# Letting VectorE share GpSimd's products and bias rows, loading masks first, and choosing a planner's urgencies anew, in a four-block attention kernel

## The chip, the cores and the metric

The kernel runs on one core of a Trainium2 chip. The metric is the device time of one execution in microseconds (us), given as the median of several runs. A profile of one further execution comes with it. Its engines are PE (TensorE's matmuls), PEld (TensorE's weight loads), DVE (VectorE), ACT (ScalarE), POOL (GpSimd) and SP (SyncE, which here only issues transfers).

## The reference

Eight sequences of 128 tokens with 256 features go through four transformer blocks, L0 to L3, all in fp32. `ctx_2048` is a second set of eight sequences of the same shape. Cut to what matters:

```
L0: x += attention(norm(x), ctx, mask)    # 16 heads of 16, boolean mask over keys
    x += mlp(norm(x))                     # 256 -> 1024 -> 256
L1: attention of x over [ctx, x]          # integer mask over keys, no norm ahead of it
    x = that and an MLP of its norm
L2: x += wide_attention(norm(x), ctx)     # twice; 16 heads of 128, learned bias key/value
    x += mlp(norm(x))
L3: x += attention(norm(x), norm(x), ltor_mask)
    x += attention(norm(x), ctx, cross_mask)
    x += mlp(norm(x))

# L3's attention:
scores = einsum(q, k) / sqrt(16)
scores = scores * mask - 10000.0 * (1.0 - mask)
probs  = softmax(scores)
return einsum(probs, v)
```

Each attention and each MLP ends with a bias row of 256 numbers that is added to every token.

## The kernel before

**Threads.** The eight sequences are cut into five threads, T0 to T4, of 1, 1, 2, 2 and 2 sequences (`SIZES`). A thread is a chain of Python generators, `blocks(T)`, that goes through L0, L1, L2 and L3. Threads run beside each other, so that TensorE has the products of one while the others are in a softmax or a norm. At most three are in the first two blocks, and three in the wide one. The last thread is cut in two parts, one sequence each, for L3 (`BY_BATCH`, `Part`).

**The order.** No engine's order is written by hand. While the program is built, the class `Plan` plays the kernel through: it keeps a clock (`now`), a time until which each engine is taken (`until`), and a list of what the generators ask for. A generator yields `op(engine, f)`, or a sum of two of these where either engine may do the work. When an engine comes free, `_choose` gives it the most urgent thing that names it (the lowest number, then the oldest) and calls `f`, which emits the instructions. Engines are asked in the order PE, POOL, ACT, DVE, SP. How long an instruction takes on the planner's clock comes from `_weight`, which also tells whether a DVE instruction shares SBUF's port with POOL: then the planner starts it only when POOL is done (`_end`). Where TensorE would idle, the planner may put in a matmul on `ident` whose result nobody reads (`idle_work`).

**Urgencies.** The numbers in `U` belong to kinds of work (`'norm'`, `'mask'`, `'k'`, `'softmax'`, `'load'`, ...), and those in `LATE` are added for each thread and stage. Together they make the order. A wrong guess of the planner costs time on the chip, as each engine keeps to the emitted order.

**Transfers.** `load` asks SP for a transfer, or SP or ACT where it is marked `early`. `dma` places its landing on the planner's clock: `dma_until` is the time at which the transfers asked so far are through, 2500 ns at first, and each KB adds 2.8 ns. `inputs` asks for `x`, `ctxT` and the columns of biases and scales (`cols`) with urgency -3. `key_bias` loads the mask over keys with -1, on SP alone; from it DVE makes `hs`, `ms` and `kss`, ACT or POOL write biases into `k`, and DVE adds the keys of `ctx` to these.

**L3's softmax**, `by_pairs`, works on 128 queries x four heads x 128 keys at a time (a tile `t` of 128x512):

```
DVE   t = scores * mask                 (scores in PSUM)
POOL  t = t + (mask - 1) * -10000
DVE   mn = min of t
ACT   t = exp(mn - t), sums into sm     (four instructions)
DVE   sm = 1 / sm
POOL  t = t * sm                        ("the product with the inverse sums")
PE    transposes of t, then t times v
```

L2's softmax, `after_scores`, has such a product on POOL too; the profile names both `t<-t,sm`.

**Rows of biases.** `normed` loads the bias row that a stage adds at its end into `row`; `norm` starts `add_rows`, which adds it to the residual (`x<-x,row`) on POOL. The stage's last DVE addition, `x<-mm,x`, waits for this through `row_in`. In `norm` the case `w is None` is L1's attention, which has no norm: there the transposes read the residual itself.

Nearly every instruction is recorded at line 335, the call in `Engine`; groups are told apart by tile names.

Of the kernel before, what the change touches and what calls it, by code (L numbers as in the profile page):

```python
# [62 lines left out]
FRONTS, WIDES = 3, 3  # L63
BY_BATCH = (4,)
AHEAD = [[(1, 0), (1, 1)], [], [(1, 0)], [], []]
U = {'take': 0.75, 'taken': -1, 'norm': 1.33, 'mask': 5.29, 'k': 2.24, 'q': 0.77, 'v': 3.01, 'by key': 0.17, 'softmax': 1.71, 'weights': 1.17, 'pairs': 0.21, 'out': 0.57, 'mlp norm': -0.18, 'mlp 1': 2.92, 'mlp 2': 3.41, 'wide norm': 1.02, 'wide k': 3.4, 'wide q': 3.13, 'wide v': 5.44, 'wide s': 4.05, 'wide': 0.43, 'ahead': 3.67, 'load': -0.56, 'early': 0.98}
LATE = [(4.59, -1, -1, -0.66, 1.03, -1, 2.77, 3.05, 3.1, 3.0, 2.25, 1.84, 0.92), (16.8, 0.32, 4.0, 6.02, 1.18, -1, 3.37, 3.57, 8.14, 4.15, -0.94, 0.09, 0.94), (2.67, 10.11, 4.03, 1.81, 2.31, 3.16, 3.3, 3.73, 4.79, 13.74, 3.59, 9.93, 9.83), (4.81, 12.33, 4.01, -1, -0.06, 1.37, 3.1, -0.03, 1.5, 1.56, 0.96, -0.5, -1), (1.56, 2.64, -0.58, -0.46, 1.42, -0.16, 4.41, 1.29, 0.75, -1, -1, 3.81, -0.53)]


class Event:  # L70
# [14 lines left out]
class Plan:  # L85
# [12 lines left out]
    def __init__(self):  # L98
        self.now = 0
        self.seq = 0  # L100
        self.events = []
        self.asked = []
        self.until = {e: 0 for e in self.SEEN}
        self.weight, self.shared, self.wrote = 0, False, []
        self.idle_work = None
        self.both_until = {"DVE": 0, "POOL": 0}
        self.clock = Clock()
        self.count = 0
        self.log = []
        self.table = None  # L110
        self.dma_until = 2500
        self.live = {}

    def spawn(self, gen, urgency, after=0):
# [150 lines left out]
def _weight(eng, name, args, kw):  # L265

    aps = [x for x in (*args, *kw.values()) if isinstance(x, bass.AP)]
    sizes = [x.free_size() for x in aps]
    n = max(sizes)
    if name == "dma_start":  # L270
        return 480, False
    by_part = sum(m == 1 for m in sizes[1:]) if n > 2 else max(0, len(aps) - 2) if name == "tensor_scalar" else 0
    on_sbuf = all(x.space == bass.MemoryType.SB for x in aps)
    if eng == "PE":
        if name == "transpose":
            return 109, False
        lhsT = kw["lhsT"]
        cols = aps[0].free_size()
        if lhsT.shape[0] < P:
            return 0.539 * cols, False  # L280
        if lhsT.free_size() < P:
            return 0.494 * cols, False
        return max(225, 1.7 * cols), False
    if eng == "ACT":
        if "accum_out" in kw:
            return 385, False
        if name == "copy":
            return 61 + 0.824 * n, False
        return 127 + 0.805 * n + (35 if on_sbuf and n == 256 else 0) + (40 if isinstance(kw.get("bias"), bass.AP) else 0) + (
            90 if isinstance(kw.get("scale"), bass.AP) else 0), False  # L290
    if eng == "DVE":
        if name == "tensor_scalar" and n == 4 and len(aps) == 2 and len(args) > 5:
            return 145, False
        if name == "reciprocal":
            return 65 + 6.25 * n, False
        if name in ("bn_stats", "bn_aggr"):
            return (330 if name == "bn_stats" else 150), False
        if n <= 8:
            return 68 + 55 * max(0, len(aps) - 2) * (name == "tensor_scalar"), False
        if name in ("tensor_scalar", "tensor_copy") and on_sbuf:  # L300
            return 75 + 0.8 * n + 55 * by_part, True
        two = name in ("tensor_tensor", "scalar_tensor_tensor") and sum(
            x.space == bass.MemoryType.SB and x.free_size() > 1 for x in aps[1:]) == 2
        return 72 + 1.03 * n + 55 * by_part, two
    if name == "memset":
        return 20 + n, False
    if n <= 16:
        return 195 + 75 * by_part, False
    if name == "tensor_tensor":
        inner = any(x.ap[-1][0] == 0 for x in aps[1:])  # L310
        return 100 + (1.85 if inner else 2.3) * n, False
    return (150 + 3.0 * n, 10 + 3.6 * n, 5 * n - 20)[by_part], False
# [34 lines left out]
def op(eng, f, lat=None, table=None):  # L347
    return ((eng, 0, f, lat, table),)
# [8 lines left out]
def four_blocks(ctx: ExitStack, tc: tile.TileContext, a: dict, out: bass.AP):  # L357
# [79 lines left out]
    def dma(f, kb_, early):  # L437

        def sync():
            f(nc.sync)  # L440
            plan.weight += max(0, plan.dma_until - plan.now - 3500)

        yield op("SP", sync) + (op("ACT", lambda: f(nc.scalar)) if early else ())
        plan.dma_until = max(plan.dma_until, plan.now) + kb_ * 2.8
        yield plan.dma_until - plan.now + 2300

    def load(dst, src, kb_, early=False):
# [189 lines left out]
    def norm(T, src, e, w, b, adds, rows, hT, ready, row_done, urgency):  # L637
# [4 lines left out]
        else:  # L642
# [48 lines left out]
                    nc.vector.tensor_scalar(xn[:, i, :], src[:, i, :], y[:, i, :], z[:, i, :], ALU.mult, ALU.add)  # L691

            yield from each(*(either(lambda i=i: scaled_act(i), lambda i=i: scaled_dve(i)) for i in range(nb)))
        spawn(add_rows(adds, rows, row_done, nb), urgency)
        yield (tl, 1)
        pt = bank("tl")[:, : NC * T.nt].rearrange("p (c b k) -> p c b k", c=NC, b=nb)

# [3 lines left out]
                    nc.tensor.transpose(pt[:, c, i, :], xn[:, i, c * P : (c + 1) * P], ident)  # L701

        yield op("PE", transposes)

        def out_act(c):
            to, s = hT[:, c, :], pt[:, c].rearrange("p b k -> p (b k)")
# [21 lines left out]
    def add_rows(adds, rows, row_done, nb):  # L728
        for (dst, src, _), (r, e) in zip(adds, rows):
            yield e  # L730
            yield op("POOL", lambda: nc.gpsimd.tensor_tensor(
                dst, src, r.unsqueeze(1).to_broadcast([P, nb, D]), ALU.add))
            plan.put(row_slots)
        plan.set(row_done)

# [72 lines left out]
    def key_bias(mask, dst, hs, ks, ks_in, name, dtype, T, may_be_none):  # L808

        nb = T.nb
        raw = mask[:, 0].bitcast(dtype)[:, :, :P]
        m = mask[:, 1]
        ms = new(act, [P, 2, nb], "ms", bufs=4)
        kss = new(act, [P, 2, NC, nb], "kss", bufs=4)
        yield spawn(load(raw, a[name][:, T.tokens].rearrange("o (b k) -> o b k", k=P).partition_broadcast(P), 64 * nb), -1)
        some = new(act, [P, nb], "some", bufs=4)

        def minus():
            nc.vector.tensor_scalar(m, raw, 0.0, -BIG, ALU.is_equal, ALU.mult)
            if may_be_none:
                nc.vector.tensor_reduce(some, m, AX.X, ALU.max)
                nc.vector.tensor_scalar(some, some, -1.0, None, ALU.is_ge)
            else:
                nc.vector.memset(some, 1.0)
            for e in range(2):
                nc.vector.tensor_scalar(hs[:, e], some, half[e], None, ALU.mult)
                nc.vector.tensor_scalar(ms[:, e], some, mask_row[e], None, ALU.mult)  # L830

        def biases():
            for e in range(2):
                for c in range(NC):
                    nc.vector.tensor_scalar(kss[:, e, c], some, ks[:, e, c : c + 1], None, ALU.mult)

        yield op("DVE", minus)
        yield ks_in
        yield op("DVE", biases)
        yield from each(*(  # L840
            op("ACT", lambda e=e, c=c, b=b: nc.scalar.activation(
                dst[:, e, c, b, 0, :], m[:, b], AF.Identity, bias=kss[:, e, c, b : b + 1], scale=ms[:, e, b : b + 1]))
            + op("POOL", lambda e=e, c=c, b=b: nc.gpsimd.tensor_scalar(
                dst[:, e, c, b, 0, :], m[:, b], ms[:, e, b : b + 1], kss[:, e, c, b : b + 1], ALU.mult, ALU.add))
            for e in range(2) for c in range(NC) for b in range(nb)))
# [253 lines left out]
    def by_pairs(T, ns, scale, mask, masks, q, k, v, v_in, vb, attnT):  # L1099
# [24 lines left out]
        def softmax(s, b, r, mn, sm, ts):  # L1124
# [12 lines left out]
            def exps():  # L1137
# [5 lines left out]
            yield op("ACT", exps, None, EXP)  # L1143
            yield op("DVE", lambda: nc.vector.reciprocal(sm[:, r], sm[:, r]))
            yield op("POOL", lambda: nc.gpsimd.tensor_tensor(
                t, t, sm[:, r].to_broadcast([P, 4, P]), ALU.mult))

        def values(b, soft, ts, turn, next_turn):
            yield turn
# [342 lines left out]
    def inputs():  # L1492
        for T in threads:
            h = T.h
            early = h < 2
            rows = (load(T.x, a["x"][T.batches].rearrange("b p d -> p b d"), 128 * T.nb, early),
                    load(T.ctx, a["ctxT"].rearrange("(c p) t -> p c t", p=P)[:, :, T.tokens], 128 * T.nb, early))
            for f, then in zip(rows, (T.ready, ctx_in[h])):
                spawn(all_then([spawn(f, -3)], then), 0)
            if h == 0:  # L1500
                spawn(all_then([spawn(load(cols, a["cols"], 140, True), -3)], cols_in), 0)
                first = new(const, [P, 1], "first")
                spawn(asks(op("ACT", lambda: nc.scalar.activation(first, ident[:, :1], AF.Exp), None, EXP)), 9)
            spawn(blocks(T), 0)
            yield 4000 if h == 0 else 8000
# [46 lines left out]
```

## Time and profile before

| | |
|---|---|
| median of 3 runs | 1195.21 us (1195.16 to 1196.08) |
| profiled execution, its own time | 1194.78 us |
| its span, first to last instruction | 1193.0 us |
| mean granted TensorE clock | 0.993 |
| PE busy | 1150.5 us (96%) |
| DVE, ACT, POOL busy | 798.8, 596.3, 360.4 us |
| moved by the transfers | 181.09 MB, 152 GB/s on average |
| POOL `t<-t,sm`, 128x512 | 128 times, 1041 ns each |
| POOL `t<-t,mask`, 128x512 | 64 times, 1276 ns each |
| POOL `x<-x,row` | 48 times, 999 ns each, over two sizes |

A busy share is an average over the whole span; what a change in one stage is worth shows only in that stage's stretch. The digits in the profile's second part are the busy share of 40 equal slices of the span, in tenths. In a group's row the columns are the engine, the operation, the tiles written and read, shapes and count; then the busy time in us and the mean ns of one; then the time in which the engine idled just before them, and what ended it. A row of the timeline has the start and length in us, and in brackets how long the engine stood idle before it and whose end released it. SPq and ACTq are the engines' issue of transfers.

### The profile page before, as it was taken

To read this page: it belongs to the slowest core of one execution; us is meant where nothing else is said; L and a number is where in the kernel's file an instruction comes from. 1 tells how busy PE (TensorE), PEld (TensorE's weight loads), DVE (VectorE), ACT (ScalarE), POOL (GpSimd) and SP (SyncE) were. 2 spreads that over 40 slices of the span, in tenths; PEclk is the share of its full clock that TensorE was granted. 3 is DMA by queue.
4 is the path that set the end of the run, shared out by engine and by line. 5 is a ranking of instruction groups with operands and counts; after the bars stand their busy time and mean duration, and the time that the engine had idled before them with its cause. 6 is when DMAs were issued, how large, how long until landed. Compare 5 with 4: busy or idle time off the path is not lost.

```text
span 1193.0 us, 23579 instructions
## 1 busy us (share of the span) xinstructions
PE 1150.5 (96%) x8816; PEld 956.5 (80%) x8816; DVE 798.8 (67%) x2186; ACT 596.3 (50%) x1538; POOL 360.4 (30%) x446
## 2 busy tenths in 40 slices
PE   7999999999999999999999999999999999988978
PEld 6677788888888878887887878888787778877767
DVE  6867568747776586787477265556855657678972
ACT  3555455355445374557353343633553336367872
POOL 2211211223124253013202022412532226165770
PEclk8999999999999999999999999999999999998999
DMA  9754567787645554435334534446443564351120
GB/s 299 219 162 136 160 201 214 238 273 229 190 143 196 152 185 145 135 112 147 117 116 141 165 106 145 124 131 187 138 137 122 139 183 133 117 143 55 32 85 19
DMA packets 134706, 181.09 MB, mean 152 GB/s; under 512 B 8896, under 2 KB 83392, under 8 KB 134592
## 3 DMA queue, kind: packets, MB, share of 16 engines
q1 hardware_dynamic: 133344, 178.55, 48.7%
q8 instruction: 70, 1.15, 0.4%
q10 hardware_dynamic: 1248, 1.03, 0.3%
q14 instruction: 44, 0.36, 0.1%
HBM read 178.50 MB, written 1.05 MB: 151 GB/s over the span
## 4 chain that ended last, share of the span: by engine, by line
PE 79%; DVE 11%; ACT 5%; DMA 2%; issue 1%; POOL 0%; SPq 0%; ACTq 0%; POOLq 0%; DVEq 0%
PE mm L335 57%; PE tl L335 17%; PE sc L335 5%; DVE rz L335 2%; ACT kb L335 1%; DVE t L335 1%; DMA w<-in_L_wk 1%; DMA bb<-in_L_bias_v 1%; ACT t L335 1%; DVE mn L335 1%; ACT q L335 1%; DVE ry L335 1%; ACT pt L335 1%; DVE kb L335 1%; DVE q L335 1%
## 5 line engine op out<-in xcount | busy, mean ns | idle before, releaser
L335 PE MATMUL mm<-hT,w 128*128 128x256 f32 (+1 forms) x1576 | 292.4, 335 | 12.0 <-ACT kb L335 2.5
L335 PEld LDWEIGHTS mm<-hT,w 128*128 128x128 f32 x1576 | 242.8, 191 | 43.5 <-issue 8.0
L335 POOL TENSOR_TENSOR t<-t,sm 128x512 f32<-128x512 f32 x128 | 132.0, 1041 | 298.5 <-DVE sm L335 242.8
L335 PE MATMUL mm<-ctxT,w 128*128 128x256 f32 (+1 forms) x768 | 148.7, 342 | 1.7 <-DVE x L335 0.8
L335 PE MATMUL mm<-w,ctxT 128*128 128x512 f32 (+1 forms) x352 | 145.9, 542 | 4.6 <-DMA w<-in_L_v_w 2.0
L335 PEld LDWEIGHTS mm<-ctxT,w 128*128 128x128 f32 x768 | 121.7, 194 | 16.5 <-issue 3.0
L335 PE MATMUL mm<-w,at 128*128 128x256 f32 x512 | 121.5, 380 | 0.2 <-DVE kb L335 0.2
L335 PE MATMUL mm<-w,kb 128*128 128x256 f32 x512 | 119.6, 382 | 0.9 <-PE mm L335 0.8
L335 POOL TENSOR_TENSOR x<-x,row 128x256 f32<-128x256 f32 (+1 forms) x48 | 48.0, 999 | 232.7 <-ACT xn L335 108.3
L335 PEld LDWEIGHTS mm<-w,at 128*128 128x128 f32 x512 | 94.7, 190 | 16.2 <-issue 2.6
L335 ACT ACTIVATE t<-t,mn 128x128 f32<-128x128 f32 x256 | 99.5, 395 | 12.8 <-DVE mn L335 11.6
L335 PEld LDWEIGHTS mm<-w,kb 128*128 128x128 f32 x512 | 94.1, 190 | 14.6 <-PE mm L335 1.4
L335 DVE TENSOR_TENSOR x<-mm,x 128x256 f32<-128x256 f32 (+1 forms) x102 | 47.6, 466 | 82.8 <-PE mm L335 82.1
L335 POOL TENSOR_TENSOR t<-t,mask 128x512 f32<-128x512 f32 x64 | 80.2, 1276 | 63.9 <-DVE t L335 62.5
L335 PEld LDWEIGHTS mm<-w,ctxT 128*128 128x128 f32 x352 | 63.0, 192 | 42.7 <-issue 33.6
L335 POOL TENSOR_TENSOR bv<-bv,bb 128x512 f32<-128x512 f32 x40 | 50.8, 1271 | 153.2 <-DMA bb<-in_L_bias_v 137.0
L335 ACT ACT_TABLE_LOAD x60 | 77.0, 1283 | 15.5 <-PE sc L335 6.7
L335 ACT ACTIVATE at<-tl,cols 128x128 f32<-128x128 f32 x212 | 60.4, 371 | 46.5 <-PE tl L335 46.2
L335 PE MATMUL tl<-ident,t 128*128 128x128 f32 x512 | 75.5, 276 | 7.7 <-ACT pt L335 4.4
L335 ACT ACTIVATE kb<-mm,cols 128x256 f32<-128x256 f32 (+1 forms) x168 | 59.5, 422 | 43.5 <-PE mm L335 43.2
L335 PEld LDWEIGHTS tl<-ident,t 128*128 128x128 f32 x512 | 60.0, 141 | 26.0 <-issue 11.6
L335 ACT ACTIVATE t<-t 128x516 f32<-128x516 f32 x64 | 40.4, 634 | 78.4 <-DVE t L335 78.4
(124 smaller groups left out, 1851.7 us busy)
## 6 DMA issues: line engine op xcount, KB each, us to landing
w<-in_L_wk SPq DMA_DIRECT2D x40, 512.0 KB, 4.7
w<-in_L_wv SPq DMA_DIRECT2D x40, 512.0 KB, 4.1
w<-in_L_wq SPq DMA_DIRECT2D x40, 512.0 KB, 4.5
w<-in_L_wo SPq DMA_DIRECT2D x40, 512.0 KB, 4.5
bv<-in_L_bv SPq DMA_DIRECT2D x40, 256.0 KB, 4.7
bb<-in_L_bias_v SPq DMA_DIRECT2D x40, 256.0 KB, 5.7
w<-in_L_mlp_w SPq DMA_DIRECT2D x20, 512.0 KB, 4.8
w<-in_L_w_fc SPq DMA_DIRECT2D x20, 512.0 KB, 4.4
```

Of the source, the lines that this page charges most:

```text
L335: return f(*args, **kw)
```

## The change

- L3's product `t * sm` and the additions of bias rows may go to DVE as well as to POOL; the planner gives each to the one that comes free first. L2's product and L3's `t + mask` stay on POOL.
- In L1's attention, where the transposes read the residual itself, `add_rows` is started after these transposes instead of before them.
- The loads come in another order: `cols` and the masks of T0 and T1 have urgency -5, `x` and `ctxT` of T0 and T1 have -4 (the other threads' stay at -3). The masks of T0 and T1 may also be issued by ACT.
- The planner's costs: transfers are through at 3300 ns at first instead of 2500 and take 2.9 ns a KB instead of 2.8; DVE instructions on at most eight columns with all operands in SBUF (other than memset, and those priced further up) count as sharing POOL's port.
- Most numbers of `U` and `LATE` are new.

```diff
-U = {'take': 0.75, 'taken': -1, 'norm': 1.33, 'mask': 5.29, 'k': 2.24, 'q': 0.77, 'v': 3.01, 'by key': 0.17, 'softmax': 1.71, 'weights': 1.17, 'pairs': 0.21, 'out': 0.57, 'mlp norm': -0.18, 'mlp 1': 2.92, 'mlp 2': 3.41, 'wide norm': 1.02, 'wide k': 3.4, 'wide q': 3.13, 'wide v': 5.44, 'wide s': 4.05, 'wide': 0.43, 'ahead': 3.67, 'load': -0.56, 'early': 0.98}
+U = {'take': -0.25, 'taken': -0.55, 'norm': 1.74, 'mask': 6.1, 'k': 2.59, 'q': 0.08, 'v': 3.01, 'by key': 0.17, 'softmax': 1.56, 'weights': 1.17, 'pairs': 0.21, 'out': 0.57, 'mlp norm': -1, 'mlp 1': 2.92, 'mlp 2': 4.05, 'wide norm': 0.2, 'wide k': 3.4, 'wide q': 3.13, 'wide v': 5.44, 'wide s': 4.05, 'wide': 0.6, 'ahead': 3.8, 'load': 0.2, 'early': 1.82}
...
-        self.dma_until = 2500
+        self.dma_until = 3300
...
-            return 68 + 55 * max(0, len(aps) - 2) * (name == "tensor_scalar"), False
+            return 68 + 55 * max(0, len(aps) - 2) * (name == "tensor_scalar"), on_sbuf and name != "memset"
...
-        plan.dma_until = max(plan.dma_until, plan.now) + kb_ * 2.8
+        plan.dma_until = max(plan.dma_until, plan.now) + kb_ * 2.9
...
-        spawn(add_rows(adds, rows, row_done, nb), urgency)
+        if w is not None:
+            spawn(add_rows(adds, rows, row_done, nb), urgency)
...
         yield op("PE", transposes)
+        if w is None:
+            spawn(add_rows(adds, rows, row_done, nb), urgency)
...
             yield op("POOL", lambda: nc.gpsimd.tensor_tensor(
-                dst, src, r.unsqueeze(1).to_broadcast([P, nb, D]), ALU.add))
+                dst, src, r.unsqueeze(1).to_broadcast([P, nb, D]), ALU.add)) + op("DVE", lambda: nc.vector.tensor_tensor(
+                    dst, src, r.unsqueeze(1).to_broadcast([P, nb, D]), ALU.add))
...
-        yield spawn(load(raw, a[name][:, T.tokens].rearrange("o (b k) -> o b k", k=P).partition_broadcast(P), 64 * nb), -1)
+        yield spawn(load(raw, a[name][:, T.tokens].rearrange("o (b k) -> o b k", k=P).partition_broadcast(P), 64 * nb, T.h < 2), -5 if T.h < 2 else -1)
...
             yield op("POOL", lambda: nc.gpsimd.tensor_tensor(
-                t, t, sm[:, r].to_broadcast([P, 4, P]), ALU.mult))
+                t, t, sm[:, r].to_broadcast([P, 4, P]), ALU.mult)) + op("DVE", lambda: nc.vector.tensor_tensor(
+                    t, t, sm[:, r].to_broadcast([P, 4, P]), ALU.mult))
...
-                spawn(all_then([spawn(f, -3)], then), 0)
+                spawn(all_then([spawn(f, -4 if early else -3)], then), 0)
             if h == 0:
-                spawn(all_then([spawn(load(cols, a["cols"], 140, True), -3)], cols_in), 0)
+                spawn(all_then([spawn(load(cols, a["cols"], 140, True), -5)], cols_in), 0)
```

`LATE`'s tuples are left out of this diff; most of their 65 numbers move by up to 3, a few by more.

More of the change, by code (lines that the diff above doesn't have):

```diff
@@ L65 @@
 AHEAD = [[(1, 0), (1, 1)], [], [(1, 0)], [], []]
-U = {'take': 0.75, 'taken': -1, 'norm': 1.33, 'mask': 5.29, 'k': 2.24, 'q': 0.77, 'v': 3.01, 'by key': 0.17, 'softmax': 1.71, 'weights': 1.17, 'pairs': 0.21, 'out': 0.57, 'mlp norm': -0.18, 'mlp 1': 2.92, 'mlp 2': 3.41, 'wide norm': 1.02, 'wide k': 3.4, 'wide q': 3.13, 'wide v': 5.44, 'wide s': 4.05, 'wide': 0.43, 'ahead': 3.67, 'load': -0.56, 'early': 0.98}
-LATE = [(4.59, -1, -1, -0.66, 1.03, -1, 2.77, 3.05, 3.1, 3.0, 2.25, 1.84, 0.92), (16.8, 0.32, 4.0, 6.02, 1.18, -1, 3.37, 3.57, 8.14, 4.15, -0.94, 0.09, 0.94), (2.67, 10.11, 4.03, 1.81, 2.31, 3.16, 3.3, 3.73, 4.79, 13.74, 3.59, 9.93, 9.83), (4.81, 12.33, 4.01, -1, -0.06, 1.37, 3.1, -0.03, 1.5, 1.56, 0.96, -0.5, -1), (1.56, 2.64, -0.58, -0.46, 1.42, -0.16, 4.41, 1.29, 0.75, -1, -1, 3.81, -0.53)]
+U = {'take': -0.25, 'taken': -0.55, 'norm': 1.74, 'mask': 6.1, 'k': 2.59, 'q': 0.08, 'v': 3.01, 'by key': 0.17, 'softmax': 1.56, 'weights': 1.17, 'pairs': 0.21, 'out': 0.57, 'mlp norm': -1, 'mlp 1': 2.92, 'mlp 2': 4.05, 'wide norm': 0.2, 'wide k': 3.4, 'wide q': 3.13, 'wide v': 5.44, 'wide s': 4.05, 'wide': 0.6, 'ahead': 3.8, 'load': 0.2, 'early': 1.82}
+LATE = [(4.8, 1.85, -1, 2.6, 0.57, -0.78, 2.77, 3.05, 3.1, 4.26, 0.92, 0.68, 0.92), (16.26, 0.15, 2.27, 4.87, 1.1, -1, 4.59, 3.64, 7.89, 3.63, -0.44, -1, 0.62), (2.02, 13.1, 4.03, 1.89, 2.39, 4.21, 4.35, 3.73, 5.32, 12.69, 3.59, 12.53, 12.43), (4.76, 11.96, 3.75, 0.32, -0.11, 0.19, 1.97, -0.71, -0.29, 1.07, 2.21, -0.13, 0.52), (2.69, 2.78, -0.58, -0.46, 1.42, -0.24, 5.22, 2.76, -0.37, -1, -1, 3.02, 0.65)]
 class Event:
```

## The prediction

> **What bounds the kernel now.** I read the page's first two parts first, then the busy time by stretches, then TensorE's waits, the start in order of time, and last the forms of GpSimd's instructions in the final stretch.
>
> ```profile
> PE 1150.5 (96%) x8816; PEld 956.5 (80%) x8816; DVE 798.8 (67%) x2186; ACT 596.3 (50%) x1538; POOL 360.4 (30%) x446
> PE   7999999999999999999999999999999999988978
> POOL 2211211223124253013202022412532226165770
> PEclk8999999999999999999999999999999999998999
> ```
>
> TensorE is the bound: 1150.5 of 1193.0 us busy, at nearly the full granted clock. 42.5 us are idle, and the digits put them at the two ends. POOL, at 30% of the span, reaches seven tenths only in the end. The stretches with the ends in them:
>
> ```profile
> 0.00:30.00 30.00, 22.99 (x167) 20.18 (x168) 19.03 (x83) 9.62 (x23) 8.50 (x29) 0.89 0.92 299
> 150.00:180.00 30.00, 29.83 (x300) 25.70 (x299) 20.04 (x50) 15.73 (x33) 4.86 (x5) 1.00 0.64 202
> 1050.00:1080.00 30.00, 23.92 (x193) 19.43 (x191) 22.48 (x60) 20.69 (x74) 19.66 (x23) 0.93 0.37 102
> 1110.00:1140.00 30.00, 27.57 (x317) 22.51 (x318) 27.95 (x75) 23.62 (x92) 24.05 (x25) 1.00 0.18 54
> 1140.00:1170.00 30.00, 24.93 (x216) 20.34 (x217) 21.64 (x65) 19.71 (x75) 17.11 (x16) 1.00 0.14 40
> ```
>
> Columns: the stretch, its length, busy time of PE, PEld, DVE, ACT and POOL, then clock, DMA share, GB/s. The first row loses 7.0 us. From 30 to 150 the four rows not shown lose 8.8 us. From 150 to 1050 PE loses under 9 us in 900. From 1050 on it idles 18.1 of 143 us, 3.3 of them after 1170. So some 16 us lie at the start and 18 at the end: a new plan can win there only. In the end DVE (27.95 of 30) is fuller than POOL (24.05).
>
> The start, in order of time:
>
> ```profile
> 2.24 0.47 SPq L335 DMA_DIRECT2D mask<-in_mask_b  x1
> 6.32 0.15 DVE L335 TENSOR_TENSOR rz<-mv,rv 128x1 f32<-128x1 f32 x1
> 9.61 0.35 ACTq L335 DMA_DIRECT2D x<-in_x  x1
> 9.61 0.23 DVE L335 TENSOR_SCALAR mask<-mask 128x128 f32<-128x128 uint8 x1 [3.15 <-DMA mask<-in_mask_b]
> 11.70 0.38 ACTq L335 DMA_DIRECT2D ctxT<-in_ctxT  x1
> 12.12 0.60 ACT L335 ACTIVATE xn<-x,rz,ry 128x256 f32<-128x256 f32 x1 [7.82 <-DMA x<-in_x]
> 16.87 0.87 DVE L335 SCALAR_TENSOR_TENSOR k<-mm,hs,k 128x256 f32<-128x256 f32 x2
> ```
>
> Two things hold this start. The mask of thread 0, 16 KB, is issued seventh or eighth and lands 7.4 us later, at 9.6; everything that builds `k` from it follows, to 16.87. And `xn` has its inputs at 6.47, but stands in ACT's queue behind two loads of thread 1, which go only at 9.61 and 11.70, as older transfers land.
>
> The end:
>
> ```profile
> L335 POOL TENSOR_TENSOR t<-t,mask 128x512 f32<-128x512 f32 x32 | 40.1, 1278 | 14.4 <-DVE t L335 14.4
> L335 POOL TENSOR_TENSOR t<-t,sm 128x512 f32<-128x512 f32 x32 | 32.9, 1040 | 14.5 <-DVE sm L335 13.7 <-DVE ry L335 0.5
> ```
>
> These are POOL's groups from 1050 on: half of all L3 softmaxes lie in the last 12% of the span.
>
> **The change, part by part.**
>
> *L3's products on GpSimd or VectorE.* Of 128 products `t<-t,sm` of 1041 ns, 64 are L3's (8 batches, two attentions, four each), 32 of them in the end. What VectorE takes for one is not in the trace. The nearest rows are 128x512 with one operand in PSUM, `t<-tl,t`, at 687 ns, and 128x256 with both in SBUF, `attnT<-tm`, at 486. I take 0.68, ends 0.53 and 1.04. The Trainium skill's GPSIMD Engine Reference (section 3.1) has GpSimd 1.96 times as slow on a tensor_tensor, which would make it 1041/1.96 = 0.53 (an estimate); the row decides.
>
> How many move? The planner asks POOL before DVE when both are free. From 1050 to 1150 POOL is busy 74.2 and DVE 86.2 of 100 us. POOL busy with DVE free is then about 0.74 x 0.14 = 0.10 of the time, POOL free 0.26, so 0.10/0.36 = 28% go to DVE: 9 of 32, ends 0 and 32.
>
> What is one worth? Here a rule speaks against the change. The trace, in the end:
>
> ```profile
> 1071.69 1.27 POOL L335 TENSOR_TENSOR t<-t,mask 128x512 f32<-128x512 f32 x1
> 1071.75 1.22 DVE L335 TENSOR_TENSOR rz<-ry 128x1 f32<-128x1 f32 x1
> ```
>
> A one-column DVE instruction, 0.16 us elsewhere, lasts as long as the POOL one beside it. The Trainium skill's SBUF — State Buffer, "Who interferes with whom", says why: a VectorE instruction with two SBUF inputs and a GpSimd one that reads SBUF exclude each other for the whole instruction. A product on DVE is such an instruction. Counted by busy rows alone, nine moved products take 9 x 1.04 = 9.4 us off POOL; under the lock POOL stands still 0.68 of each, so its queue shortens by 9 x 0.36 = 3.2, and DVE gains 9 x 0.68 = 6.1 us of work where it is fullest. I take the lock. Beyond it, each move shortens one chain (product, transposes, `pt`, weighted sum) by 0.36 us, and by POOL's queue where up to seven additions stand ahead. POOL is not always last: PE's named waits in the end are for `pt` (10.1 us over ACT and DVE), behind which these products stand. I take -2 us, ends -6 and +8 (rival 1). The 32 earlier products lie under PE's full row: zero, ends -1 and +1; without that cover 0.36 us each.
>
> *Rows of biases.* 53 additions on POOL (`x<-x,row`, 727 ns at 128x256, 1271 at 128x512), eight of them in the end, 6.9 us. They are needed only by the DVE addition that ends the block, an attention or MLP later; that distance hides them. On DVE one costs 0.42 to 0.68 by `x<-mm,x` (420 and 684). If the planner puts one in front of a score's `t<-sc,mask`, that chain is later by as much: zero, ends -1 and +2. In L1's block, which has no norm, the additions are now asked for after the transposes of `x`, so they start later; they still have the whole attention: zero.
>
> *Masks and columns first.* Two mask loads (16 KB each) and `cols` (109 KB) go to the front for threads 0 and 1, and masks may use ACT's queue. At the 299 GB/s of the first 30 us, 125 KB are 0.4 us: `x` lands at about 4.0 instead of 3.6, and the statistics behind it shift by as much. The mask lands at about 4, not 9.6. Its chain on DVE (`mask` 9.61 to `kss` 11.45, 1.8 us) then falls into the stretch where DVE waited anyway, though it could sit before the norm's own 2.7 us. The four `k` biases would be ready near 8. With `cols` and the mask early, the transfers that held ACT's two loads end sooner, so `xn` may leave before 12.12, at best near 7; a third load of thread 1 on ACT, its mask, works the other way. PE lost 7.0 us in 30, and 24 filler matmuls on `ident` (from 1.36 on, 5.5 us) count as busy. I take -3 us, ends -6 and +3. As PE is full from 150 on, what is saved here reaches the end.
>
> *Costs in the planner, and urgencies.* The planner now lets tiny VectorE instructions wait for POOL, as the row at 1071.75 shows they do, and places transfers later (3300 instead of 2500 ns, 2.9 instead of 2.8 ns a KB). No instruction is added; the order is. The trace cannot price a new order. From above: PE's idle time outside the first 30 us and the end is 17 us (8.8 from 30 to 150, the rest later), so it can't win more than about 10. From below: an order in which one weight arrives late repeats the 2.0 us wait for `in_L_v_w` at 9.9, several times. SP waits 728 us for PE to free buffers, so transfers have room as a whole. I take -3 us (a third of the 8.8 us), ends -9 and +8.
>
> **Sum.** -2 - 3 - 3 = -8 us on the profiled execution's 1194.78, which is 1186.8. The median before, 1195.21, is 0.4 above that execution, so 1187.2; I say 1187.0.
>
> **The rivals.**
>
> 1. *DVE becomes the bound of the end* (slower). Place: 1050 to 1150. DVE is busy 86.2 of 100 us there, so 13.8 are free, or 20 products of 0.68. It decides from the 21st moved product on, or from fewer with row additions on DVE. With all 32 moved, 21.8 us less 13.8 are 8 us more, and the start gives back perhaps 3: 1195.2 + 8 - 3 = 1200. For: DVE's 27.95 of 30. Against: the planner counts DVE's load and the lock. Chance 0.15.
> 2. *The start jams in ACT's queue, and the new order makes weights late* (slower). Three loads of thread 1 in ACT's queue instead of two, each held by an older transfer: `xn` at 14 rather than 12.1, +2, and two waits like `in_L_v_w`, +4; nothing won in the end: 1201. For: the 7.82 us wait shows that this queue blocks. Against: the mask no longer ends at 9.6. Chance 0.12.
> 3. *The change does hardly what it says.* POOL is asked first, DVE is full, few products move, and the order trades waits: within 2.4 us of before, 1195. Chance 0.10.
>
> The forecast, that each end gives some of its idle time back, has 0.63. I rank it first because the idle time, the blocked queue and the lock that the planner had not counted are all in the trace, while the rivals need a plan that overloads an engine whose load it counts.
>
> **How the numbers follow.** Gains in the forecast's case run from 3 to 20 us, with about one in eight of them beyond 19: 8% below 1176. Rivals 1 and 2 lie at 1196 to 1210, about two fifths of them above 1202: 11%. So 1176 to 1202 holds 8 in 10; the forecast's own range is 1177 to 1192. A measurement of this kernel tells about 0.2% (2.4 us) from no change. Faster by more: 0.63. Within: 0.10. Slower: 0.15 + 0.12 = 0.27.
>
> **What would show it.** Right: `xn` of thread 0 before 10 us and PE over 25 of the first 30; 5 to 14 of the end's 32 products on DVE at about 0.68 us; PE idle under 14 us from 1050 to the end; PE's busy time unchanged but for filler. Wrong: DVE over 29 of 30 in the end's stretches with PE waiting for it (rival 1); ACT's loads still issued near 10 or later, or new PE waits for `w` (rival 2); all products on POOL (rival 3). A gain that lies between 150 and 1050 would refute my placing of it.

## The result, and the profile after

The changed kernel is slower: 1215.2 us, median of four runs (1212.82 to 1216.25), against 1195.64 for the kernel before on the same chip. The ratio is 1.0158, 95% interval 1.0141 to 1.0175. The forecast was 1187.0, with 1176 to 1202 as its range. The profiled execution took 1216.25 us with a span of 1213.7 and a mean granted clock of 0.989.

The page's first two parts:

```profile
span 1213.7 us, 23649 instructions
PE 1163.7 (96%) x8868; PEld 966.6 (80%) x8868; DVE 801.5 (66%) x2176; ACT 622.0 (51%) x1582; POOL 334.4 (28%) x414
PE   7889999999999999999999999999999999989888
POOL 2212011222422223113201052204511521255650
PEclk8999999999999999999999999999999999999999
```

TensorE's share is still 96%, and yet it has more to do: 8868 matmuls instead of 8816. The 52 extra ones are fillers, `mm<-ident` and `tl<-ident`, which the planner puts in where it sees TensorE idle. The two groups in before, then in after:

```profile
L335 PE MATMUL mm<-ident 128*128 128x128 f32 x56 | 11.6, 353 | 1.6 <-POOL ident masks.py:199 1.4
L335 PE MATMUL tl<-ident 128*128 128x128 f32 x16 | 3.4, 343 | 3.9 <-DVE pt L335 3.9
```

```profile
L335 PE MATMUL mm<-ident 128*128 128x128 f32 x100 | 18.9, 336 | 3.2 <-DVE q L335 1.6 <-POOL ident masks.py:199 1.4
L335 PE MATMUL tl<-ident 128*128 128x128 f32 x24 | 4.7, 332 | 0.5 <-DVE hT L335 0.5
```

So the 20.7 us of longer span divide as follows. TensorE is idle for 1213.7 - 1163.7 = 50.0 us instead of 42.5: +7.5. Fillers, which are idle time that counts as busy: 23.6 - 15.0 = +8.6. The same useful work takes 1140.1 us instead of 1135.5: +4.6, as much as the lower clock would give by itself (0.989 against 0.993 is 0.4%, or 4.6 us of 1140).

The stretches (length, busy time of PE, PEld, DVE, ACT, POOL, clock, DMA share, GB/s): first the one of before from 30 to 60, which the prediction doesn't show, then those of after.

```profile
30.00:60.00 30.00, 27.97 (x320) 19.98 (x319) 26.24 (x67) 16.37 (x30) 7.81 (x9) 1.00 0.70 216
```

```profile
0.00:30.00 30.00, 21.97 (x150) 18.55 (x154) 15.42 (x74) 9.70 (x23) 7.71 (x27) 0.83 0.95 316
30.00:60.00 30.00, 26.72 (x264) 20.04 (x257) 20.39 (x64) 14.86 (x29) 8.10 (x11) 0.94 0.59 170
150.00:180.00 30.00, 29.36 (x308) 25.50 (x307) 22.56 (x69) 19.92 (x38) 4.85 (x8) 1.00 0.49 158
1080.00:1110.00 30.00, 26.20 (x250) 21.81 (x249) 24.61 (x77) 24.32 (x86) 17.20 (x23) 0.94 0.27 76
1110.00:1140.00 30.00, 25.52 (x224) 21.92 (x223) 27.71 (x64) 18.27 (x69) 16.42 (x16) 0.97 0.17 54
1140.00:1170.00 30.00, 25.08 (x281) 20.65 (x281) 26.52 (x72) 21.20 (x89) 19.21 (x21) 0.96 0.15 45
```

The first 30 us, which were to rise over 25, fell from 22.99 to 21.97 (6.7 of them filler), and the next 30 fell from 27.97 to 26.72. In the end POOL is relieved (16.42 instead of 24.05 between 1110 and 1140, where after runs some 12 to 16 us behind), and TensorE isn't the fuller for it: from 1050 to the end it idles 19.4 us, where before idled 18.1.

The start, in order of time:

```profile
0.74 0.38 SPq L335 DMA_DIRECT2D mask<-in_mask_b  x1
4.32 0.23 DVE L335 TENSOR_SCALAR mask<-mask 128x128 f32<-128x128 uint8 x1 [1.56 <-DMA mask<-in_mask_b]
5.58 0.42 DVE L335 BATCH_NORM_STATS2 st<-x 128x6 f32<-128x256 f32 x1
8.49 2.05 PE L335 MATMUL mm<-ctxT,w 128*128 128x128 f32 x8 [2.36 <-DMA w<-in_L_k_w]
11.16 0.35 ACTq L335 DMA_DIRECT2D x<-in_x  x1
13.99 0.37 ACT L335 COPY v<-mm 128x256 f32<-128x256 f32 x1 [9.78 <-PE mm L335]
14.25 0.60 ACT L335 ACTIVATE xn<-x,rz,ry 128x256 f32<-128x256 f32 x1
14.41 3.79 PE L335 MATMUL mm<-ctxT,w 128*128 128x128 f32 x16 [0.46 <-ACT v L335]
14.76 1.64 ACT L335 ACTIVATE k<-mask,kss,ms 128x128 f32<-128x128 f32 x4
17.99 0.61 PE L335 MATMUL tl<-ident,xn 128*128 128x128 f32 x2
19.22 0.87 DVE L335 SCALAR_TENSOR_TENSOR k<-mm,hs,k 128x256 f32<-128x256 f32 x2
```

The mask lands at 4.3 as forecast, instead of 9.6. What was to follow from it does not. TensorE's first product waits 2.36 us for its weight and starts at 8.49, where before's started at 6.64. ACT is again held by loads of thread 1 (until 11.16), then takes the copy of `v` ahead of `xn`, so that `xn` starts at 14.25 instead of 12.12. TensorE puts sixteen matmuls of L2's keys (3.79 us) ahead of `xn`'s transposes, which were at 12.78 and are at 17.99. `k` is written at 19.22, not 16.87: `mask`, `ms` and `kss` are there at 8.7, but ACT writes the biases into `k` only from 14.76 on, behind `xn`.

The products and rows from 1050 on:

```profile
L335 DVE TENSOR_TENSOR t<-t,sm 128x512 f32<-128x512 f32 x8 | 6.4, 797 | 0.1
L335 POOL TENSOR_TENSOR t<-t,mask 128x512 f32<-128x512 f32 x32 | 41.3, 1313 | 30.0 <-DVE t L335 26.3 <-DVE ry L335 3.7
L335 POOL TENSOR_TENSOR t<-t,sm 128x512 f32<-128x512 f32 x24 | 25.3, 1064 | 13.3 <-DVE sm L335 11.8 <-DVE mask L335 0.8 <-DVE ry L335 0.6
```

Eight of 32 products moved (forecast: nine); 21 of 64 over the whole run, with nine row additions. POOL, less loaded, only waits longer for VectorE's `t` (26.3 us, 14.4 before).

**Where the time went.** For each kernel I added up TensorE's useful work (matmul counts by shape, a fixed time for each shape, fillers left out) over stretches of 15 us, and read off when each kernel reaches the work that before has done at a given time. The table shows how many us later that is. It is a rough measure: other fixed times for the shapes move single entries by up to 3 us, and leave the picture as it is. The kernels other than after are those of the experiments below.

| before's time, us | 48 | 129 | 441 | 843 | 1042 | 1126 | end |
|---|---|---|---|---|---|---|---|
| after | 7.7 | 7.8 | 9.2 | 12.6 | 11.8 | 15.6 | 20.9 |
| f1: after's order, no move | 6.7 | 6.7 | 8.1 | 9.9 | 10.1 | 11.6 | 15.3 |
| r5: port cost alone | 9.1 | 6.5 | 8.7 | 28.3 | 34.0 | 48.7 | 59.0 |
| r6: transfer costs alone | 7.0 | 8.2 | 8.0 | 24.6 | 31.0 | 45.9 | 48.8 |
| r2: new urgencies alone | -0.4 | 0.4 | 8.5 | 17.5 | 22.5 | 24.0 | 36.5 |
| r8: rows alone | -1.3 | 1.1 | 7.9 | 24.5 | 24.2 | 22.9 | 30.7 |
| n1: one cost 1 ns off | 0.3 | 0.5 | 6.6 | 15.0 | 17.5 | 33.4 | 44.2 |
| p1: products, own urgencies | -0.9 | -0.6 | -1.0 | 0.5 | 0.5 | -1.2 | -2.3 |

After loses some 8 us in the first 48, 4 in the next thousand, and 9 in the end. No single wait stands behind it: TensorE's longest wait for one other instruction or transfer in after is 2.8 us, and its waits for `pt`, behind which the moved products stand, even fell from 10.6 to 6.3 us over the whole run.

### The profile page after: what moved, and what is told of

The parts are those of the page before. It is cut to its first block, busy times and chain, and to the rows that moved or that the text cites. A ratio compares the mean times of both kernels' runs of the same rounds, so it can differ in the third digit from the quotient of the medians.

```text
span 1213.7 us, 23649 instructions
## 1 busy us (share of the span) xinstructions
PE 1163.7 (96%) x8868; PEld 966.6 (80%) x8868; DVE 801.5 (66%) x2176; ACT 622.0 (51%) x1582; POOL 334.4 (28%) x414
## 4 chain that ended last, share of the span: by engine, by line
PE 84%; DVE 8%; ACT 4%; DMA 2%; issue 1%; POOL 0%; ACTq 0%; SPq 0%; DVEq 0%; POOLq 0%
PE mm L335 61%; PE tl L335 18%; PE sc L335 5%; DVE t L335 1%; ACT q L335 1%; ACT t L335 1%; DVE tm L335 1%; DMA w<-in_L_wk 1%; DVE mx L335 1%; DVE q L335 1%; DVE rz L335 1%; ACT kb L335 1%; DMA w<-in_L_k_w 1%; ACT L335 1%; DVE kb L335 0%
## 5 line engine op out<-in xcount | busy, mean ns | idle before, releaser
L335 PE MATMUL mm<-hT,w 128*128 128x128 f32 (+1 forms) x1576 | 293.8, 335 | 10.9 <-DVE q L335 2.2
L335 POOL TENSOR_TENSOR t<-t,sm 128x512 f32<-128x512 f32 x107 | 112.3, 1054 | 300.2 <-DVE sm L335 230.2
L335 POOL TENSOR_TENSOR x<-x,row 128x256 f32<-128x256 f32 (+1 forms) x42 | 41.4, 986 | 290.9 <-ACT xn L335 138.1
L335 ACT ACTIVATE at<-tl,cols 128x128 f32<-128x128 f32 x204 | 57.9, 370 | 48.9 <-PE tl L335 48.7
L335 ACT COPY pt<-tl 128x512 f32<-128x512 f32 x79 | 45.6, 584 | 68.5 <-PE tl L335 68.5
L335 ACT ACTIVATE kb<-mm,cols 128x128 f32<-128x128 f32 (+1 forms) x168 | 59.2, 422 | 39.6 <-PE mm L335 39.3
```

Source lines behind the costliest of these rows:

```text
L335: return f(*args, **kw)
```

## The experiments

The medians are in us, with the ratio to the kernel before measured on the same chip and its 95% interval. The theory that stood at the end: the order that the planner emits costs the time, and not the operations, the loads or the engines that the change names. Its chief rival: the edits cost what they say, through VectorE's load, the lock, or late loads.

### The order kept, one part of the change at a time

**f1_all_pool**: the kernel after in its own order, with the moved products and rows issued on POOL.

```diff
+        self.moved = Engine(nc.gpsimd, plan, "DVE")
...
-                dst, src, ..., ALU.add)) + op("DVE", lambda: nc.vector.tensor_tensor(
+                dst, src, ..., ALU.add)) + op("DVE", lambda: nc.moved.tensor_tensor(
...
-                t, t, ..., ALU.mult)) + op("DVE", lambda: nc.vector.tensor_tensor(
+                t, t, ..., ALU.mult)) + op("DVE", lambda: nc.moved.tensor_tensor(
```

> The changed kernel with every engine's order kept as planned, but the 21 products and 9 row additions that it puts on VectorE are issued on GpSimd at the same places. Theory O (the new order itself costs the time, the engine of these 30 instructions hardly matters): 1212 to 1218 us, within 3 us of the changed kernel. Theory D (VectorE became the bound of the end): 5 to 9 us less than the changed kernel, 1206 to 1210. Theory S (the start lost it): as the changed kernel, 1215.

Measured: 1210.7, ratio 1.0134 (1.0109 to 1.0159). Without any operation moved, 15 of the 20 us remain. The other 4.5 are partly the clock: f1's runs with 0.990 and 0.994 took 1215.83 and 1209.64 to 1211.1, after's with 0.989 and 0.994 1216.25 and 1212.82. At like clock the moves cost 0 to 3 us.

**f4_t4_dve**: before's order, and thread 4's products on VectorE.

```diff
+        self.moved = Engine(nc.vector, plan, "POOL")
...
-            yield op("POOL", lambda: nc.gpsimd.tensor_tensor(
+            yield op("POOL", lambda: (nc.moved if T.h == 4 else nc.gpsimd).tensor_tensor(
```

> The kernel before with its order kept, but all 32 products of thread 4's L3, which lie in the end, are issued on VectorE instead of GpSimd. Theory D: VectorE's end is full, 5 to 9 us slower than before, 1200 to 1204. Theory O: within 3 us of before, 1192 to 1198, as each chain is 0.1 to 0.4 us shorter and VectorE about as much later.

Measured: 1197.4, ratio 1.0012 (1.0002 to 1.0023). Its group in the stretch from 1050 on:

```profile
L335 DVE TENSOR_TENSOR t<-t,sm 128x512 f32<-128x512 f32 x16 | 11.1, 711 | 0.0
```

Sixteen products moved, not the 32 that I had expected: two sequences, two attentions, four each; the stretch's other sixteen belong to other threads. They cost VectorE 0.71 us each and the kernel 0.2 to 2.8 us; at like clock it is rather more (four runs at 0.994 have a median of 1196.8, before's three 1193.5). Moving products neither gains in a kept order nor hurts much; the 21 moves from which rival 1 was to decide were not reached.

**f2_masks_first**: before's order, with thread 0's `cols` and mask issued ahead of all other loads.

```diff
+    tc.nc.scalar.dma_start(out=cols, in_=a["cols"])
+    tc.nc.sync.dma_start(out=mask4[:, 0:1]..., in_=a["mask_b"]...)
```

> The kernel before with its order kept, but the columns and thread 0's mask are issued ahead of x and ctxT, as in the changed kernel. Theory S (masks and columns first delay x and the first weights): 2 to 6 us slower than before, 1198 to 1201. Theory O: within 2 us of before, 1194 to 1197, since ACT's queue holds the norm until about 12 us anyway; a gain of 2 to 5 us would mean that the early mask frees ACT's two loads, as the prediction had it.

Measured: 1195.09, ratio 0.9999 (0.9990 to 1.0008). The mask lands at 4.2, but VectorE takes it only at 7.95, behind the norm, as the kept order says. `x` lands later, and its statistics, which wait for it, start at 5.37 (3.61 in before); `xn` starts at 11.30 (12.12), `k` is written at 17.38 (16.87). In a kept order the early loads are worth nothing, and cost nothing.

**f3_masks_later**: after's order, with `cols` issued after `x` and thread 0's mask after the first weights.

```diff
-... partition_broadcast(P), 64 * nb, T.h < 2), ...
+... partition_broadcast(P), 64 * nb, T.h < 2, 6 if T.h == 0 and name == "mask_b" else None), ...
...
-load(cols, a["cols"], 140, True)
+load(cols, a["cols"], 140, True, 2)
```

> The changed kernel with its order kept, but thread 0's columns are issued after x, and its mask after the four first weights, as before. Theory S: 3 to 6 us faster than the changed kernel, 1209 to 1212. Theory O: within 2 us of the changed kernel, 1213 to 1217, as the order of TensorE's first products stays.

Measured: 1216.47, ratio 1.0169 (1.0148 to 1.0190), no better than after. By itself this is a weak test: `x` lands at 3.6 again, but after's order has VectorE work on the mask first, so the statistics of `x` start at 10.21, later than in after (5.58). `xn` still starts 0.85 us earlier, at 13.40. Together with f2 it says that the early loads aren't what costs the start.

**s1_norm_first**: after's order, with thread 0's `xn` ahead of the copy of `v` and its transposes ahead of the sixteen matmuls (a held-back emission in `norm`, `v`'s copy and the wide keys).

> The kernel after, with two things moved by hand in its emitted order: in thread 0's first block ACT writes xn ahead of the copy of v, and TensorE transposes xn ahead of the sixteen wide-key matmuls (3.79 us) that stood before it. Nothing else differs, not the loads either. Theory O (the emitted order costs the time; in the start it is this place where the copy and the matmuls stand before the norm): the changed kernel is some 8 us behind the kernel before by 75 us, and this gives back 2 to 6 of them: 1209 to 1213. Rival L (the start is late because x and the first weights land later, 5.6 instead of 3.6 us and 8.35 instead of 6.4): the norm earlier only uncovers the next wait, 1214 to 1217, within 0.15% of the kernel after's 1215.2.

Measured: 1214.18, ratio 1.0165 (1.0146 to 1.0185). Its start:

```profile
11.74 0.60 ACT L335 ACTIVATE xn<-x,rz,ry 128x256 f32<-128x256 f32 x1 [7.53 <-DMA w<-in_L_wv]
13.89 0.64 PE L335 MATMUL tl<-ident,xn 128*128 128x128 f32 x2
18.12 0.80 ACT L335 ACTIVATE hT<-tl,cols 128x128 f32<-128x128 f32 x2
18.62 1.28 PE L335 MATMUL mm<-hT,w 128*128 128x128 f32 x8 [1.91 <-ACT hT L335]
```

The transposes come 4.1 us earlier, but `hT`, which reads them, stands in ACT's order behind `k` and `kb` and waits until 18.12; the product with `hT` starts 1.5 us earlier than in after (20.11), and by 48 us the lag is 7.7 again. My claim that this one place costs the start fell. The loss is in the order of several engines together; which rows carry it is not settled further.

### One part of the change, planned anew

| kernel | edit against its parent | expected | measured | ratio, interval |
|---|---|---|---|---|
| r1_old_urgencies | after, with before's `U` and `LATE` | below | 1238.97 | 1.0362 (1.0344 to 1.0380) |
| r2_new_urgencies | before, with after's `U` and `LATE` | below | 1231.44 | 1.0295 (1.0280 to 1.0310) |
| r4_products | before, with the choice of engine for products | below | 1197.34 | 1.0012 (1.0001 to 1.0023) |
| r5_port_cost | before, with the port cost | below | 1253.28 | 1.0483 (1.0449 to 1.0517) |
| r6_dma_cost | before, with 3300 and 2.9 | below | 1244.49 | 1.0420 (1.0393 to 1.0446) |
| r8_rows | before, with the two edits to the rows | below | 1226.14 | 1.0271 (1.0249 to 1.0292) |

```diff
# r1, r2: lines 66 and 67 exchanged
# r4, r8: the change's own lines for the products, for add_rows
# r5
-            return 68 + 55 * max(0, len(aps) - 2) * (name == "tensor_scalar"), False
+            return 68 + 55 * max(0, len(aps) - 2) * (name == "tensor_scalar"), on_sbuf and name != "memset"
# r6
-        self.dma_until = 2500
+        self.dma_until = 3300
-        plan.dma_until = max(plan.dma_until, plan.now) + kb_ * 2.8
+        plan.dma_until = max(plan.dma_until, plan.now) + kb_ * 2.9
```

**r1**

> The changed kernel with U and LATE of the kernel before; all else, the planner's new costs, loads and choices, as changed. Theory P (the planner's own clock foretells the loss: it ends at 1156.9 us for before and 1176.2 for the changed kernel, both some 39 below the chip's time, and at 1208.6 for this one): 1240 to 1250 us. Theory U (the new urgencies are what loses): 1193 to 1200. Theory M (the machine does something that the planner doesn't see): near 1215.

**r2**

> The kernel before with the new U and LATE and nothing else. Theory P: the planner's clock ends at 1188.7, so 1222 to 1232 us; the new numbers fit only the new costs, as the old ones fit only the old. Theory U: 1210 to 1218, the whole loss and no more. Theory M: 1195.

**r4**

> The kernel before with only the choice of engine for L3's products. Theory P: the planner's clock ends at 1164.9, 8 later than before's, so 1200 to 1207 us. Theory U: 1190 to 1196, the choice can only help. Theory D (VectorE the bound of the end): 1200 to 1204, but with VectorE over 29 of 30 us busy in the end and TensorE waiting for it.

**r5**

> The kernel before with only the one line changed that lets tiny VectorE instructions wait for GpSimd on the planner's clock. Theory P: that clock ends at 1214.8; less what the new waits add to it without being new on the chip (the chip had them before), 1230 to 1252 us: one cost line upsets an order whose numbers were chosen for another. Theory U: 1193 to 1198, a more truthful cost does no harm. Theory M: 1195.

**r6**

> The kernel before with only the planner's two transfer costs changed (3300 instead of 2500 ns, 2.9 instead of 2.8 ns a KB); no instruction, load or urgency differs, only the order that comes out. Theory P (the urgencies fit the costs they were chosen with, and any changed cost upsets the order): the planner's own clock ends 41 us later, at 1198.3, so 1228 to 1242 on the chip. Rival Q (these costs are nearer to the chip, so an order made with them loses nothing there whatever the planner's clock says): within 5 us of 1195.

**r8**

> The kernel before with only the change's two edits to the bias rows: each addition may go to VectorE as well, and in L1's attention it is asked for after the transposes. Theory P: the planner's clock ends at 1182.5 instead of 1156.9, so 1213 to 1225 on the chip, though the additions themselves are at most 53 x 1.27 us of work on engines with room. Rival (the planner's clock is off here, and the rows cost what they weigh): within 3 us of 1195.

Five of these are worse than the change itself. The cost edits add no instruction to the kernel's work, and each alone costs about 50 us; the new urgencies alone cost 36. Together they cost less: the new urgencies bring the new costs from 1239 (r1) back to 1215. So the urgencies go with the costs that they were chosen with, and what was lost reads as a fit; r4 alone keeps it. The table of lags adds one thing: the kernels in it with the changed port or transfer costs are 7 to 9 us late at 48 us already, the others (r2, r8, n1) not. So the start's 8 us go with the cost edits, though not with one wait: r6 has its product with `hT` at 13.02, far ahead of before's 18.17, and is as late by 48. The new order of the loads was not planned alone.

### An edit without meaning

Do the cost edits hurt by what they say, or would any edit do so?

**n1_one_ns**: before, one planner cost 1 ns lower. **n2_after_one_ns**: after, the same cost 1 ns higher.

```diff
# n1
-            return 68 + 55 * max(0, len(aps) - 2) * (name == "tensor_scalar"), False
+            return 67 + 55 * max(0, len(aps) - 2) * (name == "tensor_scalar"), False
# n2
-            return 68 + 55 * max(0, len(aps) - 2) * (name == "tensor_scalar"), on_sbuf and name != "memset"
+            return 69 + 55 * max(0, len(aps) - 2) * (name == "tensor_scalar"), on_sbuf and name != "memset"
```

> The kernel before with one planner cost 1 ns lower (67 instead of 68 ns for a VectorE instruction on at most eight columns): an edit with no meaning on the chip, which only makes the planner choose anew. Theory N (the urgencies fit one exact set of numbers; any edit that touches the planner's arithmetic, meaningful or not, gives an order without that fit): the planner's clock ends at 1201.7 instead of 1156.9, so 1232 to 1246 on the chip. Rival M (the cost edits hurt through what they say, waiting tiny instructions and later transfers): within 5 us of 1195.

> The kernel after with the same planner cost 1 ns higher (69 instead of 68). Theory N: its urgencies fit its own numbers alone, the planner's clock ends at 1203.0 instead of 1176.2, so 1232 to 1246 on the chip, 17 to 31 us over the kernel after. Rival M: within 5 us of 1215.

Measured: n1 1240.74, ratio 1.0395 (1.0364 to 1.0425); n2 1233.86, ratio 1.0313 (1.0283 to 1.0344). One nanosecond costs before 46 us, and after 19. n1's busy time, its fillers and its stretches:

```profile
PE 1179.8 (95%) x8944; PEld 976.9 (79%) x8944; DVE 788.5 (64%) x2163; ACT 610.9 (49%) x1538; POOL 360.4 (29%) x446
```

```profile
L335 PE MATMUL mm<-ident 128*128 128x128 f32 x184 | 38.1, 335 | 4.1 <-POOL ident masks.py:199 1.4 <-DVE sm L335 1.1
```

```profile
0.00:100.00 100.00, 87.31 (x867) 70.88 (x868) 73.64 (x235) 47.68 (x92) 24.48 (x55) 0.95 0.72 219
100.00:550.00 450.00, 436.13 (x3533) 366.64 (x3532) 305.62 (x853) 219.26 (x485) 111.62 (x149) 1.00 0.59 179
550.00:1050.00 500.00, 491.81 (x3259) 404.76 (x3258) 302.95 (x778) 240.39 (x599) 138.85 (x151) 1.00 0.44 134
```

Before has 87.26, 441.11 and 497.20 us of TensorE work in these three. n1's operations on ACT and POOL are the same in number (1538, 446), and its first 100 us are before's. In the middle, where I had called TensorE full, it idles 10.4 us more; of the 44 us that it is late, 27 come after 1042. With the `tl<-ident` group (2.8 us), fillers grow from 15.0 to 40.9 us over the run. So an edit needn't say anything to cost as much as the cost edits do. This doesn't clear them of the 8 us at the start, which n1 doesn't lose: what they say may have a part in these.

### Can the moves gain with an order of their own?

**p1_products_searched**: before with the choice of engine for the products (r4), and urgencies searched for that code on the planner's clock.

> The kernel before with the choice of GpSimd or VectorE for L3's products alone, and urgencies searched for it (planner's clock 1160.4; with before's own urgencies 1164.9). Theory N: 1160.4 + 38 = 1198, at worst 1204, so near before, and not the 1215 of the kernel after: the move itself is neutral once an order is fitted to it, and gains nothing. Rival G (the move frees GpSimd's queue in the end, and a fitted order shows it): under 1192.

Measured: 1193.63, ratio 0.9987 (0.9977 to 0.9998). It is 21.6 us faster than after and 1.5 faster than before, under the 0.2% that I had set as what can be told from no change. The clock can account for it: p1's twelve runs have a median clock of 0.996, before's fifteen one of 0.991, and at 0.996 p1's four took 1193.4 to 1194.1, before's one 1192.7. The move of products gains nothing. A reason shows in its own row:

```profile
L335 DVE TENSOR_TENSOR t<-t,sm 128x512 f32<-128x512 f32 x19 | 18.0, 953 | 0.1
```

A moved product takes VectorE 953 ns on average (986 in r4), hardly less than POOL's 1041. Five of the 19 take 680 to 691 ns; the other fourteen take 780 to 1524, and each of these began while an instruction of POOL was running. Not run: urgencies searched for the whole change, which would tell whether all of its 20 us can be won back.

**i1_better_urgencies**: before's code, other `U` and `LATE`.

> The kernel before, with none of the change's edits, and with other urgencies, found by a search on its own planner's clock, which ends at 1155.2 instead of 1156.9. Theory P as a way to a better kernel: -1.7 us on the chip, 1193.7. Rival R (the planner's clock predicts the chip only to several us, as the other replanned kernels lie 30 to 43 us above it, so a gain of 1.7 is luck): anything from 1188 to 1202.

Measured: 1199.77, ratio 1.0044 (1.0028 to 1.0059): slower, where the planner's clock promised 1.7 us. Over the replanned kernels the chip lies 30 to 46 us above that clock:

| | before | after | r4 | r8 | r2 | r6 | n1 | n2 | r1 | r5 | p1 | i1 |
|---|---|---|---|---|---|---|---|---|---|---|---|---|
| planner's end | 1156.9 | 1176.2 | 1164.9 | 1182.5 | 1188.7 | 1198.3 | 1201.7 | 1203.0 | 1208.6 | 1214.8 | 1160.4 | 1155.2 |
| chip | 1195 | 1215 | 1197 | 1226 | 1231 | 1244 | 1241 | 1234 | 1239 | 1253 | 1194 | 1200 |

It tells a bad order from a good one (after ends 19.3 later on it and 19.6 on the chip), but as its distance from the chip varies by 16 us, a difference of 2 us on it says nothing.

## Why the prediction was wrong

**The step that failed** is "Costs in the planner, and urgencies": -3, ends -9 and +8. Its working took the planner's costs at their meaning (more exact, hence a better order) and took TensorE's idle time as the stake. f1 puts the order at +15 (with all that redrew it, costs, urgencies, loads and choices, which f1 keeps together), and n1 shows that a cost edit without meaning can do as much as one with it. The prediction said itself that the trace can't price a new order, and gave it a gain all the same. The upper end, +8, was built from one late weight "several times". A bound from the idle time holds for a gain at most (no run came near it), and for a loss there is none. "PE is full from 150 on" says that this order leaves no gap there; n1's order opens one, and its lag grows by 17 us between 129 and 1042. A full row doesn't cover a moved order. Which waits carry the 15 us stays open; f1's lag grows by 6.7 us up to 48, by 3.4 from there to 1042, and by 5.2 in the end, in many short pieces.

**Masks and columns first**, -3: the mask's landing (4.3) was right; `x` lands at 5.5, +1.9 us where I had +0.4. The gain did not come: f2 shows 0 for the loads alone. The 8 us that after loses by 48 go with the cost edits (the lag table), which the term did not contain. That `xn` might leave near 7 was wrong by ACT's queue: again held by thread 1's loads, to 11.16, as the prediction's own counter-argument had it, and then by the copy of `v`, to 14.25.

**L3's products**, -2: the number that moves (9, measured 8) and the undisturbed time (0.68, measured 0.68 to 0.69) were right. The lock that the Trainium skill's SBUF — State Buffer ("Who interferes with whom") describes is seen in after on both sides; POOL's rows, then VectorE's:

```profile
1144.25 1.65 POOL L335 TENSOR_TENSOR t<-t,mask 128x512 f32<-128x512 f32 x1 [0.72 <-DVE t L335]
1148.54 0.72 POOL L335 TENSOR_TENSOR x<-x,row 128x256 f32<-128x256 f32 x1
```

```profile
1144.09 0.68 DVE L335 TENSOR_TENSOR t<-t,sm 128x512 f32<-128x512 f32 x1
1148.72 1.09 DVE L335 TENSOR_TENSOR t<-t,sm 128x512 f32<-128x512 f32 x1
```

POOL's addition of 1.27 us takes 1.65 when VectorE has begun a product 0.16 us ahead; VectorE's product takes 1.09 when POOL has begun 0.18 ahead. With such waits a product on VectorE takes 797 ns in the end and 897 over the whole run. The factor of 1.96 of the Trainium skill's GPSIMD Engine Reference (section 3.1) would have given 0.53 (an estimate); 0.68, from the trace's rows, was nearer, and still too low in company. For the bias rows, which are plain additions, that factor comes closer: 1271 ns on POOL and 682 on VectorE at 128x512, or 1.86. The worth was too large: f4, r4 and p1 put it between +2.4 and -1.5, at like clock between 0 and +3, with no gain to be told from nothing.

**Rows of biases**, 0: nine of 53 went to VectorE. As operations they cost nothing that f1 could show; as an edit of the plan they cost 31 us alone (r8), which the term did not hold.

**The rivals.** VectorE did not become the bound (27.71 of 30 in the fullest of the end's stretches). Rival 2 had the right side and, at the start, the right signs: `xn` at 14 (14.25), and one wait for a weight (2.36 us for `in_L_k_w`). But it had half a mechanism: its +6 was these waits, and f3 and s1 show that undoing the loads or `xn`'s wait gives nothing back. Rival 3, that the order trades waits within 2.4 us, was nearest in kind and far too small in size. None of the three priced a new order at 20 us. One slip in the working changed nothing: gains of 3 to 20 us give 1175 to 1192, not 1177 to 1192.

## What to carry to other kernels

Where a planner or a search makes the order, an edit of its costs, of what it may choose, or of its priorities can be a new draw of the whole order. Its price is then the scatter between draws (here 0 to 58 us over a dozen single draws), whether or not the edit means anything on the chip; an edit that means nothing shows how large it is. To judge an operation's move, keep the order and change the engine alone. Idle time bounds what a new order can win and says nothing of what it can lose; count fillers as idle.

## What the runs showed of the hardware

The lock between VectorE and POOL works in either direction: the later instruction took 0.38 and 0.41 us longer (1.65 instead of 1.27, 1.09 instead of 0.68), most of the 0.52 and 0.54 us for which the earlier one still ran. With two small loads ahead of it `x` landed 1.9 us later (1.8 in f2), of which 0.46 are its later issue (1.19 instead of 0.73); 125 KB at 299 GB/s would explain 0.4, and the rest stays open. And the same program varies with the granted clock from run to run: before took 1191.58 us at 0.997 and 1198.09 at 0.990, a spread wider than anything that the moves themselves did.
